# Four convolution layers in one kernel: transposes before a stage's first product, another share of evictions, and the last layer's gates spread over more stages

## The chip, the cores and the metric

The kernel runs on one core of a Trainium2 chip. The metric is the time of one execution on the device in microseconds (us); it is a median of several runs. TensorE (PE) multiplies, VectorE (DVE), ScalarE (ACT) and GpSimd (POOL) do the elementwise work, SyncE (SP) and POOL issue the DMA transfers.

## The reference

The input x is 4 images of 256 channels and 56 x 56 pixels in fp32. Four layers follow each other, each of the form x = x + layer(group_norm(x)) with 32 groups of 8 channels.

- Layers 0 and 2 are involutions: a 1x1 product reduces 256 channels to 64, a second one makes 49 weights (7 x 7) per pixel for each of 16 channel groups, and each channel is the sum of its 7 x 7 neighbourhood with these weights.
- Layer 1 is two 3x3 convolutions with batch norms.
- Layer 3 is a pair of gates: with xn the normed input, it adds xn * (cf + sf). cf is one number per channel (a sigmoid of a 256 x 256 product), sf one number per pixel (a small Fourier transform of the mean over the channels).

```python
# layer 3
x_cft = x * cf[:, :, None, None]
x_sft = x * sf[:, None, :, :]
return x_cft + x_sft
```

## The kernel before

All work is on 128 partitions, one block of 128 channels of one image ("unit", b and cb) at a time; the 8 units of an involution layer run in order. The order of instructions on every engine is the order of the Python program (`in_order`), so each engine works down its own queue; pieces of other work are put between by hand, as generators whose steps are attached to numbered places.

A unit of an involution layer has two stages.

**Tap stage** (`tap_matrices`, L560 to L599). 32 chunks, n = 0 to 31. Each has six matmuls (L571) into one PSUM buffer of two banks; there are four such buffers, and every other use of PSUM in the layer takes one too. The chunk is then written, with a bias added, to the tap matrices kt: by ACT in six operations (L582) when n % 3 is 0, else by DVE in one (L589). After chunk n the list `hooks[n]` is run: steps of the group norm for the next layer (`norm_steps`, L200: a DVE aggregate, a small matmul L207, four DVE operations, a matmul L218, a power on POOL L139 that DVE's shift L222 waits for), the channel mean, and the gates' factors.

**Column stage** (loop L1069). Seven columns of 8 pixels. For each, `apply` makes 56 small matmuls (L613) of a window xw with kt, into two PSUM buffers, which ACT and DVE add up (`un`, L628, L633); then `next_windows` (L388) makes the window three columns ahead: seven transposes (L398) of a strip of the normed input into a PSUM buffer, a copy by ACT (L399) and four DMA transfers that shift rows within SBUF (L405, L407); `next_strip` (L362) prepares the strip after it. `early[tx]` and `late[tx]` are run before and after column tx.

**Gates** (layer 3, inside layer 2's loop). When both blocks of an image have left layer 2, `gate_factors` (L711) makes cf and sf in the hooks of the following unit: weights are loaded into a dead part of the image's block (L716), cf is a product with a sigmoid (L730), sf goes to DRAM (L763). The image's output is then made in 14 chunks of 8 rows (`gate_chunk`, L768, j = 0 to 6 for both cb): a load gx (L777), for cb = 0 also a load of sf broadcast to all partitions (L774), and after a `yield` four operations on POOL (L780 to L787) and the store to the output (L788). Two cursors walk over the list of chunks: `next_load` runs a chunk's first step, `next_gate` its second.

```python
xn = xs * rstd + shift          # L780, POOL
xs = xs * scale + bias          # L785, POOL (scale = 1 + cf * rstd, bias = cf * shift)
xn = xn * sf                    # L786, POOL
xs = xs + xn                    # L787, POOL, then the store L788
```

For images 0 to 2 the gates of image b - 1 run while image b is in layer 2: two loads after column 1 of the unit cb = 0, a gate and a load after its columns 2 to 6, three of each in the next unit's tap stage (n = 16, 22, 28), and one after its columns 0 to 5. The last image's gates have code of their own at the end. `gx` has three buffers, `sfb` two.

Of the kernel before, what the change touches and what calls it, by code (L numbers as in the profile page):

```python
# [16 lines left out]
P = 128  # L17
# [54 lines left out]
def net_kernel(  # L72
# [207 lines left out]
    def involution_layer(layer, xin, xout, red, span, sb, xs_of, ahead=None, pending=None):  # L280

        with ExitStack() as es:
# [23 lines left out]
            if layer == 0:  # L306
                load(0, 0, (2, 2, 2, 1))
                load(0, 1, (2, 2, 2, 1))

                nc.scalar.copy(norm_sb[:, 3, B - 1, 1, :], mhalf)  # L310

            red_sb = wpool.tile([P, NB, 2, R], F32, name="red_sb")

# [69 lines left out]
            def window(ty):  # L383

                k, j = divmod(ty, TY)
                return (0, NSB, 2 * NSB - 1)[j] + k

            def next_windows():  # L388

                if len(xws) == len(columns):  # L390
                    return
                flat = strips[len(xws)].rearrange("p h w -> p (h w)")
                xw = work.tile([Q, NTY, P], F32, name="xw", bufs=NXW)
                xws.append(xw)

                ps = two_banks().rearrange("p i n -> p (i n)")
                for k in range(NSB):
                    nc.tensor.transpose(ps[:Q, k * P : (k + 1) * P], flat[:, k * Q : (k + 1) * Q], ident_sb)  # L398
                nc.scalar.copy(xw[:, :NSB, :], ps[:Q, : NSB * P].rearrange("q (n c) -> q n c", n=NSB))  # L399

                n = NSB - 1
                for j in range(1, TY):
                    cut = TY * QX * j
                    at = window(j)
                    nc.sync.dma_start(xw[: Q - cut, at : at + n, :], xw[cut:Q, 0:n, :])  # L405
                    eng = nc.sync if layer == 2 or j == 1 else nc.gpsimd
                    eng.dma_start(xw[Q - cut : Q, at : at + n, :], xw[:cut, 1 : 1 + n, :])  # L407
# [152 lines left out]
            def tap_matrices(b, cb, hooks):  # L560
# [3 lines left out]
                for n in range(GB // 2 * TP // PB):  # L564
                    gp, pb = divmod(n, TP // PB)
                    ps = two_banks()
                    for k in range(PB):
                        py, px = divmod(pb * PB + k, TX)
                        z0 = ZF - py * QX - px
                        for i in range(2):  # L570
                            nc.tensor.matmul(  # L571
                                ps[:Q, i, k * NT : (k + 1) * NT],
                                z_sb[i * R : (i + 1) * R, cb * GB // 2 + gp, z0 : z0 + Q],
                                hp[i * R : (i + 1) * R, py, px].rearrange("p a t -> p (a t)"),
                                start=True,
                                stop=True,
                            )
                    g0, p0 = 2 * gp, pb * PB
                    if n % 3 == 0:
                        for i in range(2):  # L580
                            for k in range(PB):
                                nc.scalar.activation(  # L582
                                    kt[:, g0 + i, pb, :, k],
                                    ps[:Q, i, k * NT : (k + 1) * NT],
                                    AF.Identity,
                                    bias=zb_sb[:, cb * GB + g0 + i, p0 + k : p0 + k + 1],
                                )
                    else:
                        nc.vector.tensor_tensor(  # L589
                            kt[:, g0 : g0 + 2, pb],  # L590
                            ps[:Q, :, : PB * NT].rearrange("q i (k t) -> q i t k", k=PB),
                            zb_sb[:, cb * GB + g0 : cb * GB + g0 + 2, p0 : p0 + PB]
                            .unsqueeze(2)
                            .to_broadcast([Q, 2, NT, PB]),
                            ALU.add,
                        )
                    for h in hooks.get(n, ()):
                        h()
# [69 lines left out]
            def channel_mean(b, cb):  # L668
# [39 lines left out]
                nc.sync.dma_start(m2_of[cb], m_dram[b][cb].rearrange("j (r w) -> (j r) w", w=W))  # L708
                yield

            def gate_factors(b):  # L711


                w3_sb = [dead(b, 1, 4 * CR * W + ci * C, C) for ci in range(NB)]
                for ci in range(NB):
                    nc.sync.dma_start(w3_sb[ci], w3[ci * P : (ci + 1) * P])  # L716
                cf = small.tile([P, NB], F32, name="cf")
# [33 lines left out]

                ps = one_bank()
                nc.tensor.matmul(ps[:H, :W], half, cs2_sb, start=True, stop=True)
                scale = small.tile([P, NB], F32, name="gscale")
                bias = small.tile([P, NB], F32, name="gbias")
                nc.vector.tensor_mul(scale, cf, norms[3][b][0])
                nc.vector.tensor_scalar_add(scale, scale, 1.0)
                nc.vector.tensor_mul(bias, cf, norms[3][b][1])
                gate_of[b] = scale, bias
                yield  # L760
                sf = small.tile([H, W], F32, name="sf", bufs=1)
                nc.vector.tensor_copy(sf, ps[:H, :W])
# [2 lines left out]

            sf_of, gate_of = {}, {}

            def gate_chunk(b, j, cb):  # L768

                rstd, shift = norms[3][b]  # L770
                at = slice(j * CR * W, (j + 1) * CR * W)
                if cb == 0:
                    sf_of[b] = work.tile([P, CR * W], F32, name="sfb", bufs=2)
                    nc.gpsimd.dma_start(sf_of[b], sf_dram[b][j : j + 1].to_broadcast([P, CR * W]))  # L774
                sf = sf_of[b]
                xs = gx_tile()
                nc.gpsimd.dma_start(xs, xout[b][cb][:, at])  # L777
                yield
# [2 lines left out]
                    xn, xs, rstd[:, cb : cb + 1], shift[:, cb : cb + 1], ALU.mult, ALU.add  # L781
                )

                scale, bias = (t[:, cb : cb + 1] for t in gate_of[b])
                nc.gpsimd.tensor_scalar(xs, xs, scale, bias, ALU.mult, ALU.add)  # L785
                nc.gpsimd.tensor_tensor(xn, xn, sf, ALU.mult)  # L786
                nc.gpsimd.tensor_tensor(xs, xs, xn, ALU.add)  # L787
                nc.gpsimd.dma_start(ov[b, cb][:, at], xs)  # L788
                yield

# [193 lines left out]
            for u, (b, cb) in enumerate(units):  # L984
                hooks = hooks0 if u == 0 else {}
                if prev is not None:
# [2 lines left out]
                    place(hooks, norm_of(layer + 1, pb, pc, st), (2, 6, 7, 11, 12, 13))  # L989
                    if layer == 2 and u < 3:  # L990
                        g = norm_of(2, B - 1, u - 1, pending[1][u - 1])
                        place(hooks, g, (19, 20, 22, 23, 25, 26))
                    if layer == 2:
                        place(hooks, channel_mean(pb, pc), (13, 17))
                        if pc == 1:
                            place(hooks, gate_factors(pb), (17, 24, 27, 28, 30, 31))
                        elif pb == B - 1:
                            factors = gate_factors(pb)
                            place(hooks, factors, (20,))
# [1 line left out]
                            hooks.setdefault(22, []).append(last_ones)  # L1001
                            place(hooks, first_half(pb), (28, 29))
                    if layer == 2 and cb == 1 and b > 0:
                        for n in (16, 22, 28):
                            hooks.setdefault(n, []).extend((next_gate, next_load))
                if b + 1 < B:
                    n = 16 if layer == 0 else (26, 21)[cb]
# [8 lines left out]
                elif last_image:  # L1016
                    place(hooks, g2, (1,))
                    hooks.setdefault(16, []).append(ahead[0])
                kt = tap_matrices(b, cb, hooks)

                early = [[] for _ in range(NTX)]
                late = [[] for _ in range(NTX)]
# [26 lines left out]
                        early[6].append(step(g))  # L1049
                if layer == 2 and b > 0:  # L1050
                    if cb == 0:
                        chunks.extend(gate_chunk(b - 1, j, c) for j in range(NCHUNK) for c in range(NB))
                        late[1] += [next_load, next_load]
                    for tx in range(2, NTX) if cb == 0 else range(NTX - 1):
                        late[tx] += [next_gate, next_load]
                if last_image and cb == 0:
                    for tx in range(6):
# [653 lines left out]
```

## Time and profile before

| | |
|---|---|
| time, median of 3 runs | 1826.7 us (1824.32 to 1828.33) |
| span of the profiled execution | 1832.9 us |
| layer 0, layer 1, layer 2 with the gates (about) | 0 to 510, 510 to 1245, 1245 to 1833 us |
| tap matmuls L571, 6144 instructions | 392.3 us busy |
| column matmuls L613, 12544 instructions | 382.5 us busy |
| evictions of taps: ACT L582 x1056, DVE L589 x336 | 307.5 us, 319.8 us busy |
| transposes L398 x784 | 112.1 us busy |

Line numbers are those of the kernel before. A group's line in the page gives the line, the engine, the operation, the tiles written and read with their shapes and the count; then busy time, the mean of one in ns, and the idle time of the engine just before them with what ended it. In the timeline, each row is a start, a duration, and in brackets the idle time before it with its releaser. Units of layer 2 are counted from 0; in the trace their column stages begin at 1295.6, 1358.5, 1430.2, 1492.3, 1562.9, 1625.8, 1696.6 and 1763.2 us, their tap stages at 1266.1, 1327.6, 1394.8, 1464.6, 1532.0, 1598.0, 1662.3 and 1734.6.

### The profile page before, as it was taken

The numbers are of one execution on the slowest core, as the hardware profiler recorded it, in microseconds if no ns is written. First come the engines' busy times: TensorE is split into PE (matmuls) and PEld (weight loads), VectorE is DVE, ScalarE is ACT, GpSimd is POOL, SyncE is SP. The second block draws the span as 40 slices with busy tenths as digits, with TensorE's granted clock in tenths as the row PEclk, the third lists the DMA queues.
The fourth block names the chain that finished last, engine by engine and source line by source line (L and its number), as shares of the span: only waits on it lengthen the run. The fifth ranks groups of instructions, "written<-read, shape, count | busy, mean of one in ns | idle before, by whom it ended". The sixth has DMA issues, their size and how long they took to land.

```text
span 1832.9 us, 55841 instructions
## 1 busy us (share of the span) xinstructions
PE 1726.3 (94%) x24034; PEld 1518.9 (83%) x24034; DVE 1379.0 (75%) x2729; ACT 845.9 (46%) x1981; POOL 429.6 (23%) x626
## 2 busy tenths in 40 slices
PE   7999999999889999999999999997999899999888
PEld 6898889888878988998899889885877777887776
DVE  3787777776589988898888988874777677677674
ACT  3566556565533222223123212114667567576554
POOL 2333432245210000000000000000000563672681
PEclk9999999999989999999999999998999999999996
DMA  2545534454651101111111210222533665764743
GB/s 84 156 154 161 175 111 149 142 159 141 185 175 47 58 35 58 68 58 51 50 60 61 73 36 33 79 90 66 159 124 128 202 200 168 216 217 131 201 140 105
DMA packets 66003, 215.75 MB, mean 118 GB/s; under 512 B 13237, under 2 KB 20926, under 8 KB 62046
## 3 DMA queue, kind: packets, MB, share of 16 engines
q1 hardware_dynamic: 48718, 145.24, 25.3%
q0 software_dynamic: 14688, 64.78, 11.0%
q8 instruction: 189, 3.10, 0.7%
q10 hardware_dynamic: 2352, 2.18, 0.4%
q14 instruction: 56, 0.46, 0.1%
HBM read 76.30 MB, written 49.15 MB: 68 GB/s over the span
## 4 chain that ended last, share of the span: by engine, by line
PE 77%; DVE 9%; ACT 6%; DMA 4%; issue 2%; SPq 1%; POOL 0%; ACTq 0%; DVEq 0%; POOLq 0%
PE mm L1482 19%; PE ps L571 17%; PE ps L613 16%; PE mm L1400 10%; PE mm L1371 5%; PE ps L398 4%; ACT kt L582 3%; DMA xw<-xw 3%; PE ps L450 2%; DVE kt L589 2%; DVE un L633 1%; ACT xw L399 1%; ACT hp L469 1%; DVE res L1475 1%; PE ps L696 1%
## 5 line engine op out<-in xcount | busy, mean ns | idle before, releaser
L613 PE MATMUL ps<-kt,xw 126*32 126x48 f32 (+1 forms) x12544 | 382.5, 236 | 46.3 <-issue 18.8
L613 PEld LDWEIGHTS ps<-kt,xw 126*32 126x32 f32 (+1 forms) x12544 | 343.5, 122 | 91.7 <-issue 51.5
L571 PE MATMUL ps<-hp,z_sb 64*126 64x133 f32 x6144 | 392.3, 281 | 14.8 <-ACT kt L582 6.8
L571 PEld LDWEIGHTS ps<-hp,z_sb 64*126 64x126 f32 x6144 | 369.7, 187 | 33.2 <-ACT kt L582 12.2
L1482 PE MATMUL mm<-v,u_sb 128*128 128x280 f32 (+1 forms) x1728 | 385.0, 384 | 3.5 <-DVE v L1307 3.5
L589 DVE TENSOR_TENSOR kt<-ps,zb_sb 126x798 f32<-126x798 f32 x336 | 319.8, 982 | 90.4 <-PE ps L571 89.9
L1482 PEld LDWEIGHTS mm<-v,u_sb 128*128 128x128 f32 x1728 | 327.5, 190 | 57.9 <-DVE v L1307 3.8
L582 ACT ACTIVATE kt<-ps,zb_sb 126x133 f32<-126x133 f32 x1056 | 307.5, 442 | 94.6 <-PE ps L571 94.0
L1400 PE MATMUL mm<-v,u_sb 128*128 128x252 f32 (+1 forms) x936 | 212.4, 388 | 3.5 <-DVE v L1291 3.5
L1400 PEld LDWEIGHTS mm<-v,u_sb 128*128 128x128 f32 x936 | 178.0, 191 | 34.2 <-issue 3.5
L633 DVE SCALAR_TENSOR_TENSOR un<-ps,s,un 128x240 f32<-128x240 f32 x224 | 102.5, 458 | 97.0 <-ACT un L628 92.8
L1519 POOL DMA_DIRECT2D x<-xs x24 | 13.1, 547 | 683.2 <-DVE xs L1518 427.4
L633 DVE SCALAR_TENSOR_TENSOR un<-ps,par_sb,un 128x240 f32<-128x240 f32 x224 | 98.2, 457 | 90.9 <-ACT un L626 86.7
L1467 ACT ACTIVATE res<-xs,shift,norm_sb 128x1120 f32<-128x1120 f32 (+1 forms) x24 | 30.2, 1259 | 235.6 <-DVE xs L1518 107.3
L399 ACT COPY xw<-ps 126x896 f32<-126x896 f32 x112 | 101.7, 908 | 48.6 <-PE ps L398 40.8
L638 POOL TENSOR_TENSOR xs<-un,xs 128x240 f32<-128x240 f32 x112 | 72.3, 666 | 199.4 <-DVE un L633 199.4
L398 PE MATMUL ps<-ident_sb,strip_sb 128*126 128x128 f32 x784 | 112.1, 284 | 0.2 <-DVE un L633 0.2
L626 ACT ACTIVATE un<-ps,par_sb 128x240 f32<-128x240 f32 x112 | 50.3, 449 | 120.6 <-PE ps L613 115.5
L628 ACT ACTIVATE un<-ps,bn_t,s 128x240 f32<-128x240 f32 x112 | 60.2, 539 | 93.1 <-PE ps L613 89.9
L139 POOL TENSOR_TENSOR norm_sb<-norm_sb,mhalf 128x1 f32<-128x1 f32 x32 | 19.8, 620 | 344.1 <-DVE norm_sb L138 344.1
L1371 PE MATMUL mm<-xs,u_sb 128*128 128x126 f32 (+1 forms) x792 | 98.5, 277 | 1.3 <-DVE xs L1334 0.9
L1371 PEld LDWEIGHTS mm<-xs,u_sb 128*128 128x128 f32 x792 | 94.4, 191 | 2.4 <-issue 1.0
(254 smaller groups left out, 2000.6 us busy)
## 6 DMA issues: line engine op xcount, KB each, us to landing
xw<-xw SPq DMA_DIRECT2D x168, 252.0 KB
xw<-xw SPq DMA_DIRECT2D x224, 126.0 KB
xw<-xw POOLq DMA_DIRECT2D x56, 252.0 KB, 4.6
xs<-x SPq DMA_DIRECT2D x24, 560.0 KB
x<-xs POOLq DMA_DIRECT2D x8, 1568.0 KB, 8.0
xs<-x SPq DMA_DIRECT2D x8, 1568.0 KB
xs<-in_x_dram SPq DMA_DIRECT2D x6, 1568.0 KB
x<-xs SPq DMA_DIRECT2D x6, 1568.0 KB
```

The costliest lines, as they stand in the source:

```text
L398: nc.tensor.transpose(ps[:Q, k * P : (k + 1) * P], flat[:, k * Q : (k + 1) * Q], ident_sb)
L399: nc.scalar.copy(xw[:, :NSB, :], ps[:Q, : NSB * P].rearrange("q (n c) -> q n c", n=NSB))
L571: nc.tensor.matmul(ps[:Q, i, k * NT : (k + 1) * NT], z_sb[i * R : (i + 1) * R, cb * GB // 2 + gp, z0 : z0 + Q], hp[i * R : (i + 1) * R, py ...
L582: nc.scalar.activation(kt[:, g0 + i, pb, :, k], ps[:Q, i, k * NT : (k + 1) * NT], AF.Identity, bias=zb_sb[:, cb * GB + g0 + i, p0 + k : p0 ...
L589: nc.vector.tensor_tensor(kt[:, g0 : g0 + 2, pb], ps[:Q, :, : PB * NT].rearrange("q i (k t) -> q i t k", k=PB), zb_sb[:, cb * GB + g0 : cb ...
L613: nc.tensor.matmul(v[m * j : m * j + m, i, :, k * TP : (k + 1) * TP], xw[:, window(ty), m * j : m * j + m], kt[:, ng * j : ng * j + ng, :, ...
L628: nc.scalar.activation(part, o[0], AF.Identity, bias=bn["t4"][:, cb : cb + 1], scale=bn["s4"][ng][:, 0, cb : cb + 1])
L633: nc.vector.scalar_tensor_tensor(part, o[e], s, part, ALU.mult, ALU.add)
L638: nc.gpsimd.tensor_tensor(dst, u, dst, ALU.add)
L1371: nc.tensor.matmul(ps[:, co * m : (co + 1) * m], u[ci][:, co * P : (co + 1) * P], v2[:, e, : n // 2, ci * WT : (ci + 1) * WT], start=(ci = ...
L1400: nc.tensor.matmul(ps, u1_sb[:, ci, dy, k, co * P : (co + 1) * P], v[:, k, dy * NB + ci : (dy + n - 1) * NB + ci + 1 : NB, :], start=(j == 0),
L1482: nc.tensor.matmul(ps, u2_sb[:, ci, dy, k, co * P : (co + 1) * P], v[:, k, dy * NB + ci : (dy + n - 1) * NB + ci + 1 : NB, :], start=(j == 0),
```

## The change

Six edits go together:

1. `begin_windows`: the seven transposes of the window that belongs to a stage's first column are issued after the tap stage, ahead of the first column's product. `next_windows` then finds them done; for all other columns it issues them itself as before.
2. Tap chunks go to ACT when n % 3 is 2 instead of 0: 10 of 32 instead of 11, and the first two and the last two chunks are DVE's.
3. In layer 2, the steps of the last image's norm and of the gates' factors lie at other chunks: the norm's at 15, 19, 20, 24, 25, 26, the load of the gates' weights at 8 instead of 17, into buffers of its own (those of `sfb`) instead of the dead block.
4. The gates' four operations are rearranged: out = xn * (sf + cf + 1/rstd) - shift/rstd, with one product of two tensors instead of two operations on two tensors.
5. The gates' chunks: three loads in the tap stage of cb = 0 (n = 18, 20, 22), sf for the first two j after its column 0, and later ones two ahead; gate and load after columns 1, 3 and 5 instead of 2 to 6, and five of each in the next tap stage (n = 4, 10, 16, 22, 28) instead of three.
6. ACT's first operation, whose result is overwritten later, is a sigmoid instead of a copy, so that the table of functions loaded at the start is the sigmoid's.

The purpose is to have TensorE do useful work while the last tap matrices are written, to keep steps of a chain from following each other too closely, and to move the gates' transfers to the tap stages, where few others run.

```diff
@@ -307,7 +307,7 @@
                 load(0, 0, (2, 2, 2, 1))
                 load(0, 1, (2, 2, 2, 1))
 
-                nc.scalar.copy(norm_sb[:, 3, B - 1, 1, :], mhalf)
+                nc.scalar.activation(norm_sb[:, 3, B - 1, 1, :], mhalf, AF.Sigmoid)
 
             red_sb = wpool.tile([P, NB, 2, R], F32, name="red_sb")
 
@@ -385,17 +385,26 @@
                 k, j = divmod(ty, TY)
                 return (0, NSB, 2 * NSB - 1)[j] + k
 
+            begun_windows = []
+
+            def begin_windows():
+
+                flat = strips[len(xws)].rearrange("p h w -> p (h w)")
+                ps = two_banks().rearrange("p i n -> p (i n)")
+                begun_windows.append(ps)
+                for k in range(NSB):
+                    nc.tensor.transpose(ps[:Q, k * P : (k + 1) * P], flat[:, k * Q : (k + 1) * Q], ident_sb)
+
             def next_windows():
 
                 if len(xws) == len(columns):
                     return
-                flat = strips[len(xws)].rearrange("p h w -> p (h w)")
+                if not begun_windows:
+                    begin_windows()
+                ps = begun_windows.pop()
                 xw = work.tile([Q, NTY, P], F32, name="xw", bufs=NXW)
                 xws.append(xw)
 
-                ps = two_banks().rearrange("p i n -> p (i n)")
-                for k in range(NSB):
-                    nc.tensor.transpose(ps[:Q, k * P : (k + 1) * P], flat[:, k * Q : (k + 1) * Q], ident_sb)
                 nc.scalar.copy(xw[:, :NSB, :], ps[:Q, : NSB * P].rearrange("q (n c) -> q n c", n=NSB))
 
                 n = NSB - 1
@@ -576,7 +585,7 @@
                                 stop=True,
                             )
                     g0, p0 = 2 * gp, pb * PB
-                    if n % 3 == 0:
+                    if n % 3 == 2:
                         for i in range(2):
                             for k in range(PB):
                                 nc.scalar.activation(
@@ -708,10 +717,13 @@
                 nc.sync.dma_start(m2_of[cb], m_dram[b][cb].rearrange("j (r w) -> (j r) w", w=W))
                 yield
 
+            def new_sf():
+                return work.tile([P, CR * W], F32, name="sfb", bufs=2)
+
             def gate_factors(b):
 
 
-                w3_sb = [dead(b, 1, 4 * CR * W + ci * C, C) for ci in range(NB)]
+                w3_sb = [new_sf()[:, :C] if b < B - 1 else dead(b, 1, 4 * CR * W + ci * C, C) for ci in range(NB)]
                 for ci in range(NB):
                     nc.sync.dma_start(w3_sb[ci], w3[ci * P : (ci + 1) * P])
                 cf = small.tile([P, NB], F32, name="cf")
@@ -751,12 +763,13 @@
 
                 ps = one_bank()
                 nc.tensor.matmul(ps[:H, :W], half, cs2_sb, start=True, stop=True)
-                scale = small.tile([P, NB], F32, name="gscale")
-                bias = small.tile([P, NB], F32, name="gbias")
-                nc.vector.tensor_mul(scale, cf, norms[3][b][0])
-                nc.vector.tensor_scalar_add(scale, scale, 1.0)
-                nc.vector.tensor_mul(bias, cf, norms[3][b][1])
-                gate_of[b] = scale, bias
+                cfx = small.tile([P, NB], F32, name="gscale")
+                back = small.tile([P, NB], F32, name="gbias")
+                rstd, shift = norms[3][b]
+                nc.vector.reciprocal(back, rstd)
+                nc.vector.tensor_add(cfx, cf, back)
+                nc.vector.scalar_tensor_tensor(back, shift, -1.0, back, ALU.mult, ALU.mult)
+                gate_of[b] = cfx, back
                 yield
                 sf = small.tile([H, W], F32, name="sf", bufs=1)
                 nc.vector.tensor_copy(sf, ps[:H, :W])
@@ -765,14 +778,14 @@
 
             sf_of, gate_of = {}, {}
 
+            def load_sf(b, j):
+                sf_of[b, j] = new_sf()
+                nc.gpsimd.dma_start(sf_of[b, j], sf_dram[b][j : j + 1].to_broadcast([P, CR * W]))
+
             def gate_chunk(b, j, cb):
 
                 rstd, shift = norms[3][b]
                 at = slice(j * CR * W, (j + 1) * CR * W)
-                if cb == 0:
-                    sf_of[b] = work.tile([P, CR * W], F32, name="sfb", bufs=2)
-                    nc.gpsimd.dma_start(sf_of[b], sf_dram[b][j : j + 1].to_broadcast([P, CR * W]))
-                sf = sf_of[b]
                 xs = gx_tile()
                 nc.gpsimd.dma_start(xs, xout[b][cb][:, at])
                 yield
@@ -781,10 +794,12 @@
                     xn, xs, rstd[:, cb : cb + 1], shift[:, cb : cb + 1], ALU.mult, ALU.add
                 )
 
-                scale, bias = (t[:, cb : cb + 1] for t in gate_of[b])
-                nc.gpsimd.tensor_scalar(xs, xs, scale, bias, ALU.mult, ALU.add)
-                nc.gpsimd.tensor_tensor(xn, xn, sf, ALU.mult)
-                nc.gpsimd.tensor_tensor(xs, xs, xn, ALU.add)
+                cfx, back = (t[:, cb : cb + 1] for t in gate_of[b])
+                nc.gpsimd.tensor_scalar_add(xs, sf_of[b, j], cfx)
+                nc.gpsimd.tensor_tensor(xs, xs, xn, ALU.mult)
+                nc.gpsimd.tensor_scalar_add(xs, xs, back)
+                if cb == 1 and j + 2 < NCHUNK:
+                    load_sf(b, j + 2)
                 nc.gpsimd.dma_start(ov[b, cb][:, at], xs)
                 yield
 
@@ -989,11 +1004,14 @@
                     place(hooks, norm_of(layer + 1, pb, pc, st), (2, 6, 7, 11, 12, 13))
                     if layer == 2 and u < 3:
                         g = norm_of(2, B - 1, u - 1, pending[1][u - 1])
-                        place(hooks, g, (19, 20, 22, 23, 25, 26))
+                        place(hooks, g, (15, 19, 20, 24, 25, 26))
                     if layer == 2:
                         place(hooks, channel_mean(pb, pc), (13, 17))
                         if pc == 1:
-                            place(hooks, gate_factors(pb), (17, 24, 27, 28, 30, 31))
+                            place(hooks, gate_factors(pb), (8, 24, 27, 28, 30, 31))
+                            chunks.extend(gate_chunk(pb, j, c) for j in range(NCHUNK) for c in range(NB))
+                            for n in (18, 20, 22):
+                                hooks.setdefault(n, []).append(next_load)
                         elif pb == B - 1:
                             factors = gate_factors(pb)
                             place(hooks, factors, (20,))
@@ -1001,7 +1019,7 @@
                             hooks.setdefault(22, []).append(last_ones)
                             place(hooks, first_half(pb), (28, 29))
                     if layer == 2 and cb == 1 and b > 0:
-                        for n in (16, 22, 28):
+                        for n in (4, 10, 16, 22, 28):
                             hooks.setdefault(n, []).extend((next_gate, next_load))
                 if b + 1 < B:
                     n = 16 if layer == 0 else (26, 21)[cb]
@@ -1017,6 +1035,8 @@
                     place(hooks, g2, (1,))
                     hooks.setdefault(16, []).append(ahead[0])
                 kt = tap_matrices(b, cb, hooks)
+
+                begin_windows()
 
                 early = [[] for _ in range(NTX)]
                 late = [[] for _ in range(NTX)]
@@ -1049,9 +1069,8 @@
                         early[6].append(step(g))
                 if layer == 2 and b > 0:
                     if cb == 0:
-                        chunks.extend(gate_chunk(b - 1, j, c) for j in range(NCHUNK) for c in range(NB))
-                        late[1] += [next_load, next_load]
-                    for tx in range(2, NTX) if cb == 0 else range(NTX - 1):
+                        late[0] += [lambda b=b, j=j: load_sf(b - 1, j) for j in range(2)]
+                    for tx in (1, 3, 5) if cb == 0 else range(NTX - 1):
                         late[tx] += [next_gate, next_load]
                 if last_image and cb == 0:
                     for tx in range(6):
```

## The prediction

> **What bounds the kernel now.** First the page, for the engine that sets the end.
>
> ```profile
> PE 1726.3 (94%) x24034; PEld 1518.9 (83%) x24034; DVE 1379.0 (75%) x2729; ACT 845.9 (46%) x1981; POOL 429.6 (23%) x626
> PE 77%; DVE 9%; ACT 6%; DMA 4%; issue 2%; SPq 1%; POOL 0%; ACTq 0%; DVEq 0%; POOLq 0%
> ```
>
> The second line is the chain that ended last: TensorE carries 77% of it and POOL nothing. A change gains only where TensorE waits. Its timeline (start, us, what, in brackets the idle before it) shows four kinds of wait that the edits touch.
>
> ```profile
> 122.94 0.40 PE L613 MATMUL ps<-kt,xw 126*64 126x96 f32 x2
> 124.19 3.23 PE L613 MATMUL ps<-kt,xw 126*64 126x96 f32 x110 [0.85 <-ACT kt L582]
> 127.35 0.98 PE L398 MATMUL ps<-ident_sb,strip_sb 128*126 128x128 f32 x7
> 1347.93 0.35 PE L207 MATMUL ps<-mv,gavg_sb 128*128 128x1 f32 x2 [0.94 <-DVE mv L204]
> 1351.68 0.35 PE L218 MATMUL ps<-d,gavg_sb 128*128 128x1 f32 x2 [1.15 <-DVE d L215]
> 1450.45 2.90 PE L613 MATMUL ps<-kt,xw 126*64 126x96 f32 x104 [2.00 <-DMA xw<-xw]
> 1687.33 0.35 PE L723 MATMUL ps<-first,xs 128*128 128x1 f32 x2 [1.43 <-DMA xs<-in_w_dram]
> ```
>
> At the start of a column stage the first product waits 0.85 us for the last tap matrices, in all 16 units; the transposes come only after it. The other lines are a norm's steps placed too close, a late column window, and late gate weights. Next the timeline of POOL in the first image with gates, since the gates' chunks are POOL's work.
>
> ```profile
> 1433.30 0.59 POOL L774 DMA_DIRECT2D sfb<-sf  x1 [8.37 <-DMA sf<-sf]
> 1438.16 0.72 POOL L780 TENSOR_SCALAR gn<-gx,norm_sb 128x448 f32<-128x448 f32 x1 [3.17 <-DMA gx<-x]
> 1438.97 0.72 POOL L785 TENSOR_SCALAR gx<-gx,gscale,gbias 128x448 f32<-128x448 f32 x1
> 1439.65 1.14 POOL L786 TENSOR_TENSOR gn<-gn,sfb 128x448 f32<-128x448 f32 x1
> 1440.87 1.19 POOL L787 TENSOR_TENSOR gx<-gx,gn 128x448 f32<-128x448 f32 x1
> 1442.36 0.59 POOL L788 DMA_DIRECT2D out_dram<-gx  x1 [0.30 <-POOL gx L787]
> ...
> 1476.25 0.56 POOL L139 TENSOR_TENSOR norm_sb<-norm_sb,mhalf 128x1 f32<-128x1 f32 x1 [8.41 <-DVE norm_sb L138]
> ...
> 1494.96 0.55 POOL L777 DMA_DIRECT2D gx<-x  x1 [2.14 <-DMA out_dram<-gx]
> ```
>
> POOL runs ahead of TensorE: five chunks at 5.7 us each, then 8.41 us idle, because a norm's power (L139) stands next in its queue and TensorE is not that far yet. The last line is the important one: a chunk's load waits until an older store from the same buffer has landed. How long a store takes is in the answer on the store's line.
>
> ```profile
> who waited for it (us, times):
>   POOL gx L777: 5.5, 5
> DMA to landing us min/median/max: 2.3/4.3/8.3
> ```
>
> So today this wait is 5.5 us over the whole kernel. Last the sums by stretch (TensorE, its weight loads, DVE, ACT, POOL busy; clock; DMA share; GB/s): the column stages of unit 1 (no gates) and unit 2 (gates).
>
> ```profile
> 1358.50:1394.80 36.30, 35.03 (x869) 28.88 (x867) 23.40 (x56) 27.43 (x51) 0.15 (x1) 1.00 0.41 124
> 1430.20:1464.60 34.40, 29.94 (x837) 26.44 (x835) 23.66 (x51) 19.13 (x29) 25.14 (x32) 1.00 0.75 209
> ```
>
> Gates take the DMA share from 0.41 to 0.75, and unit 2's stage has 4.5 us in which TensorE is idle.
>
> **What the Trainium skill says.** "DMA: Bandwidth & Descriptors", section "Anatomy of one DMA — SWDGE (gpsimd) path": a wait on a semaphore is made by the issuing sequencer before dispatch, and a transfer takes about 2.0 us and its bytes by 436 GB/s. For 224 KB that is an estimate of 2.5 us; the trace's quiet stores took 2.3. The same page, "Issuing engines are not separate DMA queues": all queues share the 16 DMA engines. The trace agrees: beside the windows' traffic stores rise to a median of 4.3 and up to 8.3 us. "ScalarE: Activation LUTs", "What ACT_TABLE_LOAD costs": 1283 ns for the load and some 1380 ns of drain; the trace has 1283 ns at L730 and TensorE idle for 0.87 us there.
>
> **The change part by part.** *Transposes ahead of the first product.* From the last tap matmul to the bulk of the first product are 1.25 us (122.94 to 124.19). The seven transposes take 0.91 (127.35 to 128.26) and move into this gap. But with chunks 2, 5, ..., 29 on ACT, both chunks 30 and 31 are DVE's: ready at -0.62 and +0.12 us from the stage's end, 0.96 each, DVE is done at +1.3, so the product starts at +1.45. It saves 0.91 - 0.20 = 0.71 us; in the three units with gate factors three small DVE operations lie between the two chunks, and 0.36 is left. At the tap stage's start DVE now has chunks 0 and 1 beside one or two statistics of 0.6 us. With four PSUM buffers I work out 0.3 us more waiting per unit in layer 0 (about 2 us in all), and in layer 2, where today chunk 0 waits for ACT's strip (0.64 us idle), 0.3 less per unit. Layer 0: 8 x 0.71 - 2 = 3.7. Units 0 to 2 of layer 2: 0.71 + 0.71 + 0.36 + 0.6 = 2.4.
>
> *Norm steps spread out.* They remove 0.94 + 1.15 + 0.48 in unit 1 and 0.94 + 1.15 in unit 2, 4.7 us; the DVE work stays, so I take 3.7. *Sigmoid table at the start:* it replaces the load that L310 does anyway; 0.9 us gained. *Gate weights at step 8 into buffers of their own:* the waits on them, 0.61 in unit 4 and 1.79 (1.43 + 0.36) in unit 6, go.
>
> *Gate chunks.* One of two 1.15 us products becomes an addition, which the trace does not show: between nothing and L785's 0.72, I take 0.72. Now the four depend on each other, starts 0.82, 0.82, 1.23 and 1.02 us apart: 3.9 us from start to store (before: 4.2). The added wait: three loads are issued ahead into three buffers, so the load after chunk k takes the buffer of chunk k itself, whose store was issued just before. POOL stands there until that store has landed, and behind it stand the next chunk, and every sixth chunk or so a norm's power; DVE's shift waits for that, then the next tap matrices and TensorE. Per chunk: 3.9 + landing L + 0.6 for the load, and 0.53 in every other for the factors' rows. L is the unknown. Its bounds are 2.3 (quiet) and 4.8 (the median in unit 2's column stage). There will be fewer transfers per time, but the windows go on: I take 3.8 in column stages, 2.5 in quiet tap stages, 5 beside a block's store or load.
>
> From the start of unit 2's column stage: the factors' rows have landed at 7.6, the first store goes at 10.9, the next at 19.7, 28.0, 36.9 and 46.4, and the power runs at 49.5 us. Today it ran at 1476.25 - 1430.16 = 46.1. TensorE alone would need it at 42.6: seven columns of 3.2 us, six transposes of 0.92, 1.45 for the start, 2 of remaining stalls, and 11.2 to step 12. So the stage speeds up and TensorE then stands still. The same way nine more chunks (the last three without a wait) lead to the next power 65.5 us later; TensorE needs 64.5, today 67.9 in units 3/4 and 65.5 in 5/6. Sums:
> - image 0: +3.4, -2.4, and -0.7 to the next column stage;
> - image 1: 49.5 against 46.8 is +2.7, then 0.0, and -2.2 (weights, transposes);
> - image 2, without block transfers: 47.5 against 49.7 is -2.2; then the last power 61.1 us later, of which 4.2 are hidden by the means' matmuls (L860), 56.9 against 59.9, -3.0.
>
> Together -4.4. With 3.7 + 2.4 + 3.7 + 0.9 = 10.7 the change gains 15.1 us: 1826.7 - 15.1 = 1811.6 us. Each 0.1 us on L in column stages costs 8.5 x 3 x 0.1 = 2.5 us.
>
> **The rivals.** (1) POOL becomes the bound outright: L at 4.8 as now, 25 us more, 1836 us. For it: the stores' median of 4.3 over all stages. Against: sixteen POOL transfers in unit 2's column stage become about ten. (2) The store's wait is hidden: L at 2.6 or less, TensorE alone sets the pace. Then unit 2 to 7 give: stalls in column stages about 10 us less, transposes and starts 4.3, weights 2.4, a 0.8 us wait for DVE beside POOL in three units 2.4, together 19; with 10.7 the time is 1797 us. For it: stores in unit 5's and 7's column stages that landed in 2.3 to 2.7 us. Against: these had no loads around. (3) Gains and new waits cancel, L at 4.4: 1827 us.
>
> **How the numbers follow.** My forecast and its neighbourhood (L from 3.0 to 4.1) get 0.5, rival 2 gets 0.2, rival 3 gets 0.1, rival 1 gets 0.2. The limit of 0.2% is 3.7 us. Faster: 0.5 + 0.2 = 0.70; same, out of rival 3: 0.08; slower: 0.22. The range goes from rival 2, 1797, to nearly rival 1, 1834.
>
> **What would show it.** Right: the 0.85 us at L613 gone and seven transposes in the gap; no idle before L207 in unit 1; one table load; POOL's load waiting 2 to 5 us on the store just issued, in eleven chunks per image; POOL at its power in units 3, 5 and 7 without idle time before, and DVE and TensorE idle for some 5 us there; unit 2's column stage near 31.5 us. Wrong: stores that land in over 4.4 us, or a tap stage lengthened by DVE, which would be near 93% busy in layer 0 (22.55 + 0.98 of 25.3 us).

## The result

The changed kernel takes 1893.3 us (median; 1889.8 to 1896.8) against 1826.2 for the kernel before (now four runs): ratio 1.0375, 95% interval 1.0341 to 1.0410. It is slower by 67 us, where 15 us less was forecast. In the code of after, the matmuls of the column stage are L622, the transposes L396, ACT's and DVE's tap evictions L591 and L598, the channel mean L694 (DVE), L702 and L705 (TensorE); the gates have their loads at L783 (sf) and L790 (gx), four operations at L793, L798, L799, L800 and the store at L803. L139 and L222 are still the power and the shift.

### The profile page after: what moved, and what is told of

Same layout as the page of the kernel before. It is cut to its first block, busy times and chain, and to the rows that moved or that the text cites. A ratio compares the mean times of both kernels' runs of the same rounds, so it can differ in the third digit from the quotient of the medians.

```text
span 1895.0 us, 55764 instructions
## 1 busy us (share of the span) xinstructions
PE 1726.8 (91%) x24034; PEld 1514.2 (80%) x24034; DVE 1381.7 (73%) x2745; ACT 817.0 (43%) x1884; POOL 467.4 (25%) x626
## 4 chain that ended last, share of the span: by engine, by line
PE 60%; DVE 12%; POOL 12%; DMA 7%; issue 5%; ACT 2%; POOLq 0%; SPq 0%; ACTq 0%; DVEq 0%
PE mm L1501 18%; PE ps L580 11%; PE mm L1419 10%; PE ps L622 10%; DMA out_dram<-gx 6%; PE mm L1390 5%; DVE kt L598 4%; POOL gx L800 3%; POOL gx L798 3%; PE ps L396 3%; POOL gx L799 2%; DVE un L642 2%; POOL gn L793 1%; PE ps L459 1%; DVE res L1494 1%
## 5 line engine op out<-in xcount | busy, mean ns | idle before, releaser
L580 PE MATMUL ps<-hp,z_sb 64*126 64x133 f32 x6144 | 388.2, 281 | 13.0 <-DVE kt L598 4.8
L580 PEld LDWEIGHTS ps<-hp,z_sb 64*126 64x126 f32 x6144 | 367.9, 187 | 33.1 <-issue 13.2
L622 PE MATMUL ps<-kt,xw 126*32 126x48 f32 (+1 forms) x12544 | 376.9, 234 | 13.1 <-issue 6.9
L598 DVE TENSOR_TENSOR kt<-ps,zb_sb 126x798 f32<-126x798 f32 x352 | 333.2, 980 | 72.5 <-PE ps L580 72.1
L622 PEld LDWEIGHTS ps<-kt,xw 126*32 126x32 f32 (+1 forms) x12544 | 339.4, 121 | 57.3 <-issue 35.8
L591 ACT ACTIVATE kt<-ps,zb_sb 126x133 f32<-126x133 f32 x960 | 280.7, 441 | 113.5 <-PE ps L580 113.4
L396 PE MATMUL ps<-ident_sb,strip_sb 128*126 128x128 f32 x784 | 111.5, 283 | 8.2 <-POOL strip_sb L381 5.9
L396 PEld LDWEIGHTS ps<-ident_sb,strip_sb 128*126 128x126 f32 x784 | 84.9, 142 | 19.3 <-POOL strip_sb L381 7.1
```

Of the source, the lines that this page charges most:

```text
L580: nc.tensor.matmul(ps[:Q, i, k * NT : (k + 1) * NT], z_sb[i * R : (i + 1) * R, cb * GB // 2 + gp, z0 : z0 + Q], hp[i * R : (i + 1) * R, py ...
L591: nc.scalar.activation(kt[:, g0 + i, pb, :, k], ps[:Q, i, k * NT : (k + 1) * NT], AF.Identity, bias=zb_sb[:, cb * GB + g0 + i, p0 + k : p0 ...
L598: nc.vector.tensor_tensor(kt[:, g0 : g0 + 2, pb], ps[:Q, :, : PB * NT].rearrange("q i (k t) -> q i t k", k=PB), zb_sb[:, cb * GB + g0 : cb ...
L622: nc.tensor.matmul(v[m * j : m * j + m, i, :, k * TP : (k + 1) * TP], xw[:, window(ty), m * j : m * j + m], kt[:, ng * j : ng * j + ng, :, ...
```

## The profile after

The two lines of the page, busy times and the chain that ended last:

```profile
PE 1726.8 (91%) x24034; PEld 1514.2 (80%) x24034; DVE 1381.7 (73%) x2745; ACT 817.0 (43%) x1884; POOL 467.4 (25%) x626
PE 60%; DVE 12%; POOL 12%; DMA 7%; issue 5%; ACT 2%; POOLq 0%; SPq 0%; ACTq 0%; DVEq 0%
```

TensorE works as long as before (1726.8 against 1726.3 us), so what was added is waiting: 62 us between the two executions shown here, whose spans are 1895.0 and 1832.9 us. (The mean granted clock is lower, 0.954 against 0.976, but since TensorE's busy time has not grown, the clock did not slow its work.) POOL, which carried nothing of the chain, now carries 12% of it although it is busy for only 25% of the span, and DMA has gone from 4% to 7%. POOL's own work has grown by 38 us.

First the places where something was to be gained, on TensorE's timeline:

```profile
123.41 0.98 PE L396 MATMUL ps<-ident_sb,strip_sb 128*126 128x128 f32 x7
124.32 6.93 PE L622 MATMUL ps<-kt,xw 126*64 126x96 f32 x224
132.04 0.98 PE L396 MATMUL ps<-ident_sb,strip_sb 128*126 128x128 f32 x7 [0.79 <-POOL strip_sb L381]
...
1341.09 0.38 PE L207 MATMUL ps<-mv,gavg_sb 128*128 128x1 f32 x2
1416.37 0.98 PE L396 MATMUL ps<-ident_sb,strip_sb 128*126 128x128 f32 x7
```

The transposes lie in the gap and the first products follow without a wait, 0.91 us after the transposes' start (124.32 - 123.41); the forecast had put them at 1.45, behind an eviction on DVE. Two columns now run back to back, and the next transposes wait 0.79 us for a strip that POOL has not finished. L207 in unit 1 has no idle time before it, and the page has one table load (L310) instead of two. Unit 2's column stage begins at 1416.37 instead of 1430.20 us, 13.8 us earlier; 2.8 of these were there when layer 2's first tap stage began (1263.3 against 1266.1). The execution of before that is shown ran 8 us longer than that kernel's median, so a few us of such differences are noise. The sums over unit 2's column stage, columns as before (stretch and its length; TensorE, its weight loads, DVE, ACT, POOL busy; clock, DMA share, GB/s):

```profile
1416.37:1446.62 30.25, 29.74 (x836) 26.41 (x834) 22.08 (x52) 18.21 (x26) 15.49 (x17) 1.00 0.67 191
```

The stage has 0.5 us without TensorE where it had 4.5. So up to 1446.62 us all has become better. From unit 2's column start to the end the kernel takes 478.6 us (1895.0 - 1416.37) against 402.7 (1832.9 - 1430.2): the loss of 76 us lies there. The list of waits has it, in three lines (engine, line and what it waited for: us in total, times, longest):

```profile
DVE norm_sb L222 <- POOL norm_sb L139: 116.4, 15, 23.5
POOL gx L790 <- DMA out_dram<-gx: 112.7, 33, 6.7
...
PE ps L702 <- DVE mean L694: 78.2, 5, 20.5
```

Read from below: TensorE stands still five times for the channel mean, for 78 us. DVE's mean comes after DVE's shift, which waits for POOL's power. A sixth wait of the kind is at the end (18.8 us before L878, for the last power): 97 us in all. POOL meanwhile stands at a load until the last store has landed, eleven times in each image (before: 5.5 us in 5 times). The 33 of the line above are 32 of these and a short one at a change of image; the eleventh of the first image, 10.2 us, stands in the list under "issue". How these hang together is to be seen in the chain of waits, cut out from 1447 to 1474 us, each piece with start, duration and what it is:

```profile
1448.08 1.42 POOL gx L800
1449.50 0.29 issue
1449.79 3.99 DMA out_dram<-gx
1453.78 0.29 issue
1454.07 0.54 POOL gx L790
...
1454.65 0.72 POOL gn L793
1455.38 0.08 issue
1455.46 1.44 POOL gx L798
1456.89 0.07 issue
1456.97 1.15 POOL gx L799
...
1469.56 2.28 DMA out_dram<-gx
1471.84 0.29 issue
1472.13 0.54 POOL gx L790
1472.66 0.02 issue
1472.68 0.60 POOL norm_sb L139
1473.28 0.02 issue
1473.30 0.24 DVE norm_sb L222
```

Store, landing, load, four operations, store: from 1415.2 to 1475.1 us no TensorE work is part of the chain. The power follows the last load without idle time, where the kernel before has 8.41 us of it. When the power is done, DVE has stood for 13.2 us, and when the mean has come, at 1474.29, TensorE for 12.5 us.

The view of the store's line, as shown of before:

```profile
who waited for it (us, times):
  POOL gx L790: 122.9, 34
...
DMA to landing us min/median/max: 2.3/3.5/7.6
```

Over all stages the stores land sooner than before (median 3.5 against 4.3). Yet now POOL stands through most of the landings (here the 10.2 us are counted, so 34 times).

## The experiments

Theory: the loss is the wait of POOL on the store just issued, with the power behind it; its size comes from the price of a chunk's four operations and from the landing. Rivals: POOL's additions alone are the cause, whatever the order; or the loss lies in one of the edits that have nothing to do with the gates.

### The price and the wait, each and both taken away

The groups of POOL's operations in after (line, tiles, count, then busy us and mean ns) show two that the kernel before did not have:

```profile
L798 POOL TENSOR_SCALAR gx<-sfb,gscale 128x448 f32<-128x448 f32 x42 | 59.7, 1422 | 9.2 <-DMA sfb<-sf 3.8 <-DVE xs L649 1.7
L800 POOL TENSOR_SCALAR gx<-gx,gbias 128x448 f32<-128x448 f32 x42 | 59.6, 1418 | 4.1
...
L793 POOL TENSOR_SCALAR gn<-gx,norm_sb 128x448 f32<-128x448 f32 x42 | 30.2, 718 | 1.7
```

The addition of one number per partition takes twice as long as the multiplication and addition of L793. The first experiment writes both additions as multiply by one and add:

```diff
-                nc.gpsimd.tensor_scalar_add(xs, sf_of[b, j], cfx)
+                nc.gpsimd.tensor_scalar(xs, sf_of[b, j], one, cfx, ALU.mult, ALU.add)
...
-                nc.gpsimd.tensor_scalar_add(xs, xs, back)
+                nc.gpsimd.tensor_scalar(xs, xs, one, back, ALU.mult, ALU.add)
```

> The changed kernel with the gates' two additions written as a product with a column of ones and an addition (two operations in one instruction, the form of L793); the schedule stays, with its waits for stores. Theory (POOL's pace sets layer 2, and a chunk's operations and the store's landing add up): L798 and L800 fall from 1.42 to about 0.72 us, a chunk from 5.2 to 3.9 us of operations, 14 x 3 x 1.3 = 56 us of POOL less; time 1815 to 1845 us, DVE's idle time before L222 from 116 to under 50 us. Rival (the wait for the store alone makes the loss, the price of an addition hides in it): 1880 us or more. Rival (the lengthened time has nothing to do with POOL): no change from 1893 us.

Measured: 1844.0 us, ratio 1.0099 (1.0070 to 1.0127), 49 us less than after. The two groups in it:

```profile
L800 POOL TENSOR_SCALAR gx<-gx,one,gbias 128x448 f32<-128x448 f32 x42 | 31.4, 748 | 4.4
L798 POOL TENSOR_SCALAR gx<-sfb,one,gscale 128x448 f32<-128x448 f32 x42 | 31.1, 741 | 11.7 <-DMA sfb<-sf 5.6 <-DVE un L642 2.2
```

So 56.8 us of POOL's work go (119.3 - 62.5), and the time falls by 49. What is left is still slower than before, since the waits stay:

```profile
POOL gx L790 <- DMA out_dram<-gx: 124.4, 34, 6.2
...
PE ps L702 <- DVE mean L694: 38.3, 5, 10.1
```

The second experiment keeps the slow additions and takes away what makes POOL wait: only two loads are ahead, so that a load takes the buffer of the chunk before the last, whose store is older.

```diff
-                            for n in (18, 20, 22):
+                            for n in (18, 20):
                                 hooks.setdefault(n, []).append(next_load)
```

> The changed kernel with two instead of three loads issued ahead in the tap stage (n = 18, 20; the one at 22 is left out), so that a load takes the buffer of the chunk before the last one. The slow additions stay. Theory: POOL's waits for stores (112.7 us) fall to under 20 us; a chunk takes about 6.6 us, five are done some 39 us after the column stage's start, ahead of the 42.6 us at which TensorE gets to the power; the stalls before L702 (78 us) nearly go, time 1797 to 1810 us. Rival (the slow additions are the main part): above 1850 us.

Measured: 1799.1 us, ratio 0.9855 (0.9833 to 0.9878). One load fewer ahead makes the change faster by 94 us, and faster than the kernel before. No load waits for a store any more, although the stores land later than in after (median 4.2 against 3.5 us):

```profile
who waited for it (us, times):
busy tenths in 40 slices 0000000000000000000000000000000000000000
DMA to landing us min/median/max: 2.3/4.2/8.8
```

The third has both edits.

> Both edits, two-operation additions and two loads ahead. Theory: TensorE alone sets the pace in layer 2, 1795 to 1805 us; not more than 8 us less than with two loads ahead alone, since either edit alone already leaves POOL with slack there. Rival (something else than POOL holds layer 2, such as DVE's larger share of the taps or TensorE's clock): above 1826 us.

Measured: 1796.5 us, ratio 0.9846 (0.9829 to 0.9862). The same kernel ran a second time, as a partner for a later one:

> The kernel after with cheap additions and two loads ahead, a second time, as the partner of the next two. 1796 us as the first time, 0.985 of before.

Measured: 1797.6 us, ratio 0.9840 (0.9818 to 0.9862). Its waits for stores (first run of the two) and POOL's power on the timeline:

```profile
POOL gx L790 <- DMA out_dram<-gx: 7.8, 5, 2.1
...
1462.02 0.56 POOL L139 TENSOR_TENSOR norm_sb<-norm_sb,mhalf 128x1 f32<-128x1 f32 x1 [10.00 <-DVE norm_sb L138]
1526.22 0.57 POOL L139 TENSOR_TENSOR norm_sb<-norm_sb,mhalf 128x1 f32<-128x1 f32 x1 [10.44 <-DVE norm_sb L138]
```

POOL is ahead of TensorE again, with 6.2 to 12.3 us of idle time before the powers of the stages with gates, although stores land later than in after (median 4.7 against 3.5 us). The four corners together, as ratios to before:

| | three loads ahead | two ahead |
|---|---|---|
| additions of 1.42 us | 1.0375 (after) | 0.9855 |
| additions of 0.75 us | 1.0099 | 0.9846, 0.9840 |

The price costs 2.8% in the left column and 0.1%, within the intervals, in the right one. The wait costs 5.2% above and 2.5 to 2.6% below. The two do not add up: in these four kernels the price shows in the time only where the waits have used up POOL's room.

### The price alone and the wait alone in the kernel before

The other way round, on the kernel before. First only the gates' operations of after (edit 4), in the old order (the factors on DVE are left out here):

```diff
...
-                scale, bias = (t[:, cb : cb + 1] for t in gate_of[b])
-                nc.gpsimd.tensor_scalar(xs, xs, scale, bias, ALU.mult, ALU.add)
-                nc.gpsimd.tensor_tensor(xn, xn, sf, ALU.mult)
-                nc.gpsimd.tensor_tensor(xs, xs, xn, ALU.add)
+                cfx, back = (t[:, cb : cb + 1] for t in gate_of[b])
+                nc.gpsimd.tensor_scalar_add(xs, sf, cfx)
+                nc.gpsimd.tensor_tensor(xs, xs, xn, ALU.mult)
+                nc.gpsimd.tensor_scalar_add(xs, xs, back)
```

> The kernel before with edit 4 alone: the gates' operations rearranged, so the two slow additions stand in the old schedule, whose loads wait on older stores. A chunk's four operations last 4.70 us instead of 3.77. Theory (the price hurts only where POOL has no room): POOL stood idle for 8.4 us before the power, five chunks need 5 us more of it, so 0 to +6 us, 1824 to 1831 us. Rival (the additions are themselves the cause of the loss): as much as from after to after with cheap additions, +40 us or more, over 1864 us.

Measured: ratio 1.0001 (0.9985 to 1.0017). POOL's powers in the gates' tap stages of this kernel:

```profile
1472.56 0.57 POOL L139 TENSOR_TENSOR norm_sb<-norm_sb,mhalf 128x1 f32<-128x1 f32 x1 [5.59 <-DVE norm_sb L138]
1538.10 0.57 POOL L139 TENSOR_TENSOR norm_sb<-norm_sb,mhalf 128x1 f32<-128x1 f32 x1 [2.27 <-DVE norm_sb L138]
1602.82 0.57 POOL L139 TENSOR_TENSOR norm_sb<-norm_sb,mhalf 128x1 f32<-128x1 f32 x1 [3.10 <-DVE norm_sb L138]
```

In the kernel before these three have 8.41, 8.92 and 8.65 us of idle time ahead of them; the second and third, beside the first, which the prediction shows:

```profile
1544.12 0.56 POOL L139 TENSOR_TENSOR norm_sb<-norm_sb,mhalf 128x1 f32<-128x1 f32 x1 [8.92 <-DVE norm_sb L138]
1609.66 0.56 POOL L139 TENSOR_TENSOR norm_sb<-norm_sb,mhalf 128x1 f32<-128x1 f32 x1 [8.65 <-DVE norm_sb L138]
```

The slow additions have eaten 2.8 to 6.7 us of that. Only at the last power is nothing left, and TensorE waits 0.8 us for it. In the time nothing shows. The rival that makes the additions the cause by themselves, whatever the order, falls.

Then only the wait, with the old operations at their old places:

```diff
-                        late[1] += [next_load, next_load]
+                        late[1] += [next_load, next_load, next_load]
```

> The kernel before with one load more ahead (three after column 1 instead of two), so that each load takes the buffer of the store just issued; operations, places and everything else are the old ones. Theory (POOL stands at the load until that store has landed, and the power behind it stops DVE and TensorE): five chunks before the power, each with about 4 us more of waiting, 20 us less 8.4 of idle time, so +12; nine chunks to the next power at 5.7 + 4 us against 68 us today, so about +18; over three images +60 to +90 us, 1885 to 1915 us. Rival (the wait matters only with the new places of the chunks): below +15 us, under 1840 us.

Measured: 1860.9 us, ratio 1.0212 (1.0186 to 1.0238), 37 us more from one load issued earlier. That is well past the rival's 15 and short of the 60 to 90 expected. Its waits:

```profile
POOL gx L777 <- DMA out_dram<-gx: 109.7, 32, 6.8
...
DVE norm_sb L222 <- POOL norm_sb L139: 58.2, 10, 11.3
...
PE ps L693 <- DVE kt L589: 38.9, 5, 10.0
```

The last of these, in the kernel before:

```profile
PE ps L693 <- DVE kt L589: 2.7, 3, 0.9
```

The waits are those of after, one behind the other, the six powers again have no idle time ahead of them, and TensorE stands as long as it does in the kernel with cheap additions (38.3 us). The expectation put a wait into all nine chunks between one power and the next; the last three load nothing, so only six have it, and 9 x 5.7 + 6 x 4 is 75 us, 7 over the 68 of before and not 18. With its 12 for the other power that would be 57 us over three images; the rest of the miss was not followed up. (That TensorE's wait is named after L589 is DVE's queue: the eviction in front of L693 on DVE stands behind the shift.)

### What the other edits bring

All edits but those of the gates' operations and chunks (1, 2, 3 and 6 in the kernel before):

> The edits outside the gates' chunks alone: transposes ahead, ACT's share of the taps, norm and weights at other chunks, sigmoid table at the start; the chunks' operations, places and loads as before. Theory: 10.7 us from layer 0 and units 0 to 2 as in the prediction, 4.3 for transposes and starts in units 3 to 7, 2.4 for the weights: 1809 us. Rival (DVE's greater share of the taps costs what the transposes bring): 1822 to 1830 us.

Measured: 1810.4 us, ratio 0.9926 (0.9908 to 0.9945). The rival that puts the loss here falls: these edits gain some 14 us.

Edit 1 alone:

```diff
...
+                begin_windows()
+
                 early = [[] for _ in range(NTX)]
```

> The kernel before with edit 1 alone: seven transposes between a stage's last tap matmul and its first product. Theory (they fill a gap of 0.85 us that is there with the old share too, and edit 2 adds nothing to it): 0.7 to 0.9 us in each of 16 units, 11 to 14 us less, 1810 to 1813 us. Rival (the gain needs the other share): under 5 us, over 1819 us.

Measured: 1816.8 us, ratio 0.9962 (0.9949 to 0.9975), 6.9 us less: more than the rival's bound of 5, but less than the 11 to 14 expected. TensorE's waits show a new one:

```profile
PE ps L396 <- POOL strip_sb L381: 5.7, 8, 0.8
```

The gap of 0.85 us closes in the 16 units, and in eight of them 0.7 us come back one column later, because the strip for the following transposes is not ready. 16 x 0.85 - 5.7 is 7.9 us, near the 6.9.

Edits 3 and 6 alone (the sigmoid and the weights' buffers are left out here):

```diff
-                        place(hooks, g, (19, 20, 22, 23, 25, 26))
+                        place(hooks, g, (15, 19, 20, 24, 25, 26))
...
-                            place(hooks, gate_factors(pb), (17, 24, 27, 28, 30, 31))
+                            place(hooks, gate_factors(pb), (8, 24, 27, 28, 30, 31))
```

> The kernel before with edits 3 and 6 alone: norm steps spread out, gate weights loaded at chunk 8 into their own buffers, sigmoid table at the start. Theory: the waits seen before go, 3.7 to 4.7 of the norm, 2.4 of the weights, 0.9 of the table: 7 to 8 us less, 1816 to 1817.5 us. Rival (the waits return at the next place that waits for DVE): under 3 us, over 1821 us.

Measured: 1812.8 us, ratio 0.9943 (0.9924 to 0.9962), 10.4 us less; the 7 to 8 expected lie in the interval (6.9 to 13.9).

Edits 1, 3 and 6 together, with the old share and the old gates:

> The kernel before with edits 1, 3 and 6: no other share, gates as before. Theory: edits 1 (-7) and 3 with 6 (-10) add up, 17 us less than before, 1806 to 1807 us, against 1810.4 with edit 2; the difference to the kernel with old share and repaired gates chunks, 13 us, is then what edit 5 is worth when its wait is hidden. Rival (both remove the same waits): 10 us less, 1813 us or more.

Measured: 1810.4 us, ratio 0.9905 (0.9878 to 0.9933), 17 us less, in an interval from 12 to 22: 6.9 and 10.4 add up as far as this can tell, and the rival's 10 us or less are excluded.

Last edit 2, taken out of the kernel with cheap additions and two loads ahead (its partner is the second run above):

```diff
-                    if n % 3 == 2:
+                    if n % 3 == 0:
```

> The same with edit 2 taken back: chunks 0, 3, ..., 30 on ACT again, eleven instead of ten. Theory (edit 2 costs TensorE waits for DVE at the tap stage's start and gives nothing, since the transposes fill the gap with either share): 3 to 4 us faster than its partner, 1792 to 1794 us. Rival (with the other share the stage's last matrices come sooner and it pays): 3 us or more slower, 1800 us.

Measured: 1798.5 us, ratio 0.9851 (0.9829 to 0.9873), against 0.9840 (0.9818 to 0.9862) for its partner. The difference is 2 us, with an interval of some 6 us to either side: neither expectation is confirmed or excluded, and the share makes no difference that these times can tell. The traces show a small one: from its first tap matmul to its first product, unit 1 of layer 0 takes 26.6 us with the new share and 26.2 with the old. Beside the kernel with edits 1, 3 and 6 alone (0.9905), the chunks' new places with two loads ahead and cheap additions are worth about 0.5%, 10 us, with an interval of 3 to 16; the 13 expected lie in it.

The best version is thus the change with two loads ahead; with cheap additions as well it is 1.5 to 1.6% faster than before, no clear gain over the slow ones. Three loads ahead with a fourth buffer for gx was not tried.

## Why the prediction was wrong

**Right: the mechanism.** "... the load after chunk k takes the buffer of chunk k itself", POOL stands there, the power stands behind it, DVE's shift and TensorE behind that. The trace has it in this order, with 33 waits, eleven per image as written, no idle time before the six powers of the stages with gates, and standstills at the named places. Adding the wait to the kernel before, and taking it out of after, moved the time in the direction that it says (+37, -94 us).

**Right in sign, rough in size: the parts ahead of the gates.** 10.7 us were forecast to be gained by unit 2's column stage; 13.8 were, 2.8 of them (for 3.7) ahead of layer 2 and 11.0 (for 7.0) in it. That stage was put near 31.5 us; it took 30.3. Norm, table and weights were put at 3.7 + 0.9 + 2.4 = 7.0 us; alone they measured 10.4 (6.9 to 13.9). The transposes, some 10 us over all 16 units in the forecast, brought 6.9 alone: they were undone in part by a strip on POOL that no step named. The 2 us charged to edit 2 in layer 0 are too few for these times to show.

**Wrong, the larger part: "One of two 1.15 us products becomes an addition ... between nothing and L785's 0.72, I take 0.72."** The addition takes 1.42 us. The row chosen as the upper bound was one that does more (multiply and add, same size, same engine), and that this makes it dearer was taken for granted; the bound was no bound. From start to store a chunk takes 5.2 us and not 3.9 (1449.79 - 1444.56). Put into the forecast's own steps this is 5 chunks x 1.33 = 6.7 us more at the first power, 49.5 + 6.7 = 56.2; it ran 56.3 us after the start (1472.68 - 1416.37). A part of that is landings (20.1 us in this stretch where the forecast had 18.9), so the fit is in part luck. On the time the price is worth 49 us, measured by writing the addition in the other way.

**Wrong, the rest: "There will be fewer transfers per time, but the windows go on: I take 3.8 in column stages".** With cheap additions, as the forecast assumed them, the kernel took 1844 us and not 1811.6. There the first four stores ahead of the first power took, from their issue to the next load, 6.10, 5.76, 4.31 and 3.76 us in the first image, 4.85, 5.98, 3.59 and 5.52 in the second, 4.46, 5.36, 5.67 and 4.08 in the third: 4.95 on average. The forecast had 3.8, 3.8, 3.8 and 5, which is 4.1. For the 33 waits of three images the forecast's values sum up to 3 x (18.9 + 3 x 2.5 + 3 x 3.8) = 113 us. Without one of them, a wait of 7.1 us that the trace does not put down to the store, the measured 32 are 142 us, where the forecast has 110 for the same 32. This difference is as large as the 32 us that are missing; but that is worked out, no run has changed the landing alone, and it takes every microsecond of landing to reach the end, so the size of this term's share stays an estimate. The trace of before had the right number, the median of 4.8 in this very stage, and the forecast argued it away. In after the DMA share of unit 2's column stage did fall, from 0.75 to 0.67, but the twelve waits ahead of the first powers are 4.8 us there too. The Trainium skill ("DMA: Bandwidth & Descriptors", section "Anatomy of one DMA — SWDGE (gpsimd) path") leads to an estimate of 2.5 us for such a store; the quiet ones took 2.5 to 2.6 up to the next load, the others up to 6.8. As an estimate of a wait beside other traffic it is half of the 4.95 measured.

**The rivals.** Rival 1, POOL the bound outright with L at 4.8, gave 1836 us: with cheap additions this is within 8 us of 1844, so it was the right case, given 0.2. Beyond it, nothing in the forecast reached 1893, since all cases had the same price of 0.72. Rival 2, the wait hidden, gave 1797 us: the kernel with cheap additions and two loads ahead takes 1796.5 and 1797.6. That the sum fits so closely is in part luck, since its parts do not (6.9 us for the transposes, 10.4 for norm, table and weights); but TensorE's side was good enough, and what failed were the two terms of POOL.

**A condition that decides.** The forecast for the gates' part was close to a balance, 49.5 us for POOL against 42.6 for TensorE. Where POOL set the pace, 49 of the 56.8 us of the slow additions went to the end; where TensorE did, nothing measurable. That is why 0.7 us on an addition costs 49 us in the one kernel and nothing in another.

## What to carry to other kernels

A load issued as many ahead as there are buffers is not further ahead: it takes the buffer whose store was issued just before, and everything behind it in that engine's queue waits for the landing. So count, for every load, the age of the store that frees its buffer, and what else stands in that queue. A new operation's price is unknown until a row shows the same operation, even where it seems to do less than a known one; if the engine is near the bound, forecast with both, and measure it first.

## What was not expected of the hardware

On POOL, a tensor-scalar operation on 128 x 448 fp32 values that only adds one number per partition took 1413 to 1434 ns on average in the runs that have it (84 instructions each), and the same addition written as multiply by one and add took 736 to 757 ns, about as long as L793 with its multiplication and addition (718 to 752 ns). Whether this is the single operation or the addition as the first of two was not tried, so its cause stays open. From the issue of a 224 KB store to the next load into its buffer it took 2.6 us at the quietest, and 4.2 us (after) and 4.4 us (cheap additions) on average over the 32 waits named above.
